# Bilinear field pairs in fp32: each product as three float32r products of split parts, the partial sum scaled in PSUM, engine order written out by hand

## The chip, the cores and the metric

The kernel runs on one NeuronCore of a Trainium2 chip. The metric is the time of one execution on the device in microseconds (us), the median of several runs; less is better. A profile of one execution by the hardware profiler gives the spans, waits and transfers that are read below.

## What is computed

There are 32 fields of 128 numbers for each of 1024 batch rows, and one 128x128 matrix W for each of the 496 unordered pairs of fields. The reference, cut to what matters:

```python
_pairs = np.array(list(itertools.combinations(range(32), 2)))
v_i = inputs[:, I_IDX, :]                  # inputs: 1024 x 32 x 128, float32
v_j = inputs[:, J_IDX, :]
transformed = jnp.einsum('bpd,ped->bpe', v_i, W)   # W: 496 x 128 x 128
return transformed * v_j                   # 1024 x 496 x 128, float32
```

For each pair (i, j) field i is multiplied by the pair's matrix, and the result is multiplied element by element with field j. The output is 496 x 128 x 1024 float32 numbers, 260 MB, and it is by far the largest array.

## The kernel before, in words

Everything is laid out with the 128 embedding positions on the partitions. A pair is one tile of 128 partitions by 1024 batch columns. The host only transposes and permutes; on the chip the kernel walks the pairs in the order of `_pairs` (L20 to L22): j from 1 up, and for each j all i below it, so that each new j needs one new field.

- **Loads.** `load_x` (L49 to L53) brings one field, 512 KB, into a tile that stays for the whole run. `load_w` (L58 to L61) brings a chunk of eight matrices, 512 KB, into one of four buffers. The first few loads of fields go out on SyncE's (SP's) queue, the matrices and the later fields on ScalarE's (ACT's) queue. In the loop, a chunk is asked for three chunks ahead (L76, L77) and a field three groups ahead (L78, L79).
- **Products.** A pair takes a PSUM tile `po` of 1024 columns, two banks (L80, four such tiles), and two matmuls of 512 columns with fp32 operands (L81 to L88). Each of these appears in the profile as two MATMUL records on the PE.
- **Second factor and output.** VectorE (DVE) multiplies the PSUM tile by field j into half of an output tile `ot` (L93), and for every two pairs SP issues one transfer of 1024 KB to HBM (L95). There are six such output tiles. The last two pairs are done in halves (L97 to L100).
- **Order.** Nothing is written out by hand: the order on each engine is that of the program as the tile framework schedules it. The framework sets semaphores between engines from the tiles that an instruction reads and writes. ScalarE and GpSimd (POOL) compute nothing; ScalarE only issues transfers.

Of the kernel before, what the change touches and what calls it, by code (L numbers as in the profile page):

```python
# [1 line left out]

# [4 lines left out]

F32 = mybir.dt.float32
ALU = mybir.AluOpType

P = 128
NF = 32
NQ = NF * (NF - 1) // 2
BT = 1024
HB = 512
WC = 8
OC = 2


def _pairs():  # L20

    return [(i, j) for j in range(1, NF) for i in range(j)]  # L22


@with_exitstack
def kernel(
    ctx: ExitStack,
    tc: tile.TileContext,
    xt: bass.AP,
    wt: bass.AP,  # L30
    out: bass.AP,
):

    nc = tc.nc
    pairs = _pairs()  # L40

    xpool = ctx.enter_context(tc.tile_pool(name="x", bufs=1))
    wpool = ctx.enter_context(tc.tile_pool(name="w", bufs=4))
    opool = ctx.enter_context(tc.tile_pool(name="o", bufs=6))
    ppool = ctx.enter_context(tc.tile_pool(name="ps", bufs=4, space=bass.MemoryType.PSUM))

    x_sb = {}

    def load_x(f, eng, pieces=1):  # L49
        x_sb[f] = xpool.tile([P, BT], F32, tag=f"x{f}", name=f"x_{f}")  # L50
        s = BT // pieces
        for k in range(pieces):
            eng.dma_start(out=x_sb[f][:, k * s : (k + 1) * s], in_=xt[:, f, k * s : (k + 1) * s])  # L53

    nchunk = NQ // WC
    w_sb = {}

    def load_w(c, splits=(0, WC)):  # L58
        w_sb[c] = wpool.tile([P, WC, P], F32, tag="w", name=f"w_{c}")
        for a, b in zip(splits, splits[1:]):  # L60
            nc.scalar.dma_start(out=w_sb[c][:, a:b, :], in_=wt[:, c * WC + a : c * WC + b, :])  # L61

    load_w(0, (0, 1, 3, WC))
    load_x(0, nc.sync, 2)
    load_x(1, nc.sync, 2)
    load_x(2, nc.sync)
    load_w(1)
    load_x(3, nc.sync)
    load_w(2)
    load_x(4, nc.scalar)  # L70
    load_x(5, nc.scalar)

    out_v = out.rearrange("q e b -> e q b")
    ot = None
    for q, (i, j) in enumerate(pairs):
        if q % WC == 0 and q // WC + 3 < nchunk:  # L76
            load_w(q // WC + 3)  # L77
        if i == 0 and 5 < j + 3 < NF:  # L78
            load_x(j + 3, nc.scalar)  # L79
        po = ppool.tile([P, BT], F32, tag="po", name=f"po_{q}")  # L80
        for h in range(0, BT, HB):  # L81
            nc.tensor.matmul(  # L82
                po[:, h : h + HB],
                w_sb[q // WC][:, q % WC, :],
                x_sb[i][:, h : h + HB],
                start=True,
                stop=True,
            )  # L88
        r = q % OC
        if r == 0:  # L90
            ot = opool.tile([P, OC, BT], F32, tag="ot", name=f"ot_{q}")
        if q < NQ - OC:
            nc.vector.tensor_tensor(ot[:, r, :], po[:, :], x_sb[j][:, :], ALU.mult)  # L93
            if r == OC - 1:
                nc.sync.dma_start(out=out_v[:, q - r : q + 1, :], in_=ot[:, :, :])  # L95
        else:
            for h in range(0, BT, HB):  # L97
                s = slice(h, h + HB)
                nc.vector.tensor_tensor(ot[:, r, s], po[:, s], x_sb[j][:, s], ALU.mult)  # L99
                nc.sync.dma_start(out=out_v[:, q, s], in_=ot[:, r, s])  # L100


# [25 lines left out]
```

## Time and profile before

| what | value |
|---|---|
| median of 10 runs | 878.23 us (877.66 to 878.86) |
| the profiled execution, its own time | 878.86 us |
| its span, first to last instruction | 876.2 us |
| mean granted TensorE clock | 0.998 |
| PE busy | 856.8 us, 98% of the span, 1984 matmul records |
| DVE busy | 605.5 us, 69%, 498 instructions |
| POOL busy | 0.2 us |
| moved by DMA | 309.69 MB, mean 353 GB/s |
| read from HBM, written to it | 49.28 MB, 260.05 MB |

A group's line in the profile gives the source line, the engine, the operation, the tiles it writes and reads, their shapes and the count; then the busy time in us with the mean duration of one in ns; then the idle time of the engine just before these instructions and what ended it. The mean duration of a matmul record reaches past the point at which the next matmul starts, because matmuls are pipelined: the busy time divided by the count is the pace, the mean is the latency. "PEld" is the weight load, which runs beside the matmuls. The chain of work that ended last is followed back from the last instruction; "issue" in it is time in which nothing was waited for that the profile shows.

### The profile page before, as it was taken

To read this page: it belongs to the slowest core of one execution; us is meant where nothing else is said; L and a number is where in the kernel's file an instruction comes from. 1 tells how busy PE (TensorE), PEld (TensorE's weight loads), DVE (VectorE), ACT (ScalarE), POOL (GpSimd) and SP (SyncE) were. 2 spreads that over 40 slices of the span, in tenths; PEclk is the share of its full clock that TensorE was granted. 3 is DMA by queue.
4 is the path that set the end of the run, shared out by engine and by line. 5 is a ranking of instruction groups with operands and counts; after the bars stand their busy time and mean duration, and the time that the engine had idled before them with its cause. 6 is when DMAs were issued, how large, how long until landed. Compare 5 with 4: busy or idle time off the path is not lost.

```text
span 876.2 us, 5490 instructions
## 1 busy us (share of the span) xinstructions
PE 856.8 (98%) x1984; PEld 377.2 (43%) x1984; DVE 605.5 (69%) x498; POOL 0.2 (0%) x4
## 2 busy tenths in 40 slices
PE   8997899999999999999999999999999999999997
PEld 3442344444444444444444444444444444444443
DVE  4754677777777777777777777777777777777775
POOL 0000000000000000000000000000000000000000
PEclk9999999999999999999999999999999999999999
DMA  9999999989889898888988989888898988889877
GB/s 344 420 420 420 421 420 415 360 339 355 333 351 342 339 358 333 349 339 340 355 339 345 342 344 351 338 344 342 350 345 338 347 339 353 342 338 352 329 311 296
DMA packets 81898, 309.69 MB, mean 353 GB/s; under 512 B 5584, under 2 KB 5840, under 8 KB 81872
## 3 DMA queue, kind: packets, MB, share of 16 engines
q1 hardware_dynamic: 68624, 262.16, 75.3%
q10 hardware_dynamic: 13248, 47.19, 15.2%
q8 instruction: 15, 0.25, 0.1%
q14 instruction: 11, 0.09, 0.0%
HBM read 49.28 MB, written 260.05 MB: 353 GB/s over the span
## 4 chain that ended last, share of the span: by engine, by line
PE 93%; DMA 6%; DVE 0%; DVEq 0%; issue 0%; SPq 0%
PE po L82 93%; DMA x<-in_xt_dram 3%; DMA w<-in_wt_dram 2%; DMA out_dram<-ot 1%; DVE ot L93 0%; DVE ot L99 0%; DVEq L121 0%; DVEq L93 0%; SPq L95 0%
## 5 line engine op out<-in xcount | busy, mean ns | idle before, releaser
L82 PE MATMUL po<-x,w 128*128 128x512 f32 x1984 | 856.8, 594 | 13.9 <-DVE ot L93 9.9
L93 DVE TENSOR_TENSOR ot<-po,x 128x1024 f32<-128x1024 f32 x494 | 603.0, 1224 | 265.5 <-PE po L82 227.2
L82 PEld LDWEIGHTS po<-x,w 128*128 128x128 f32 x1984 | 377.2, 191 | 492.6 <-issue 470.1
L99 DVE TENSOR_TENSOR ot<-po,x 128x512 f32<-128x512 f32 x4 | 2.6, 686 | 0.9 <-PE po L82 0.9
L115 POOL MEMSET const-bfloat16-1.0<- 128x1 bf16 x1 | 0.1, 101 | 0.0
L115 POOL MEMSET const-uint8-127<- 128x1 uint8 x1 | 0.1, 101 | 0.0
L115 POOL MEMSET const-float32-0.0<- 128x1 f32 x1 | 0.1, 98 | 0.2 <-issue 0.2
L115 POOL MEMSET const-float32-1.0<- 128x1 f32 x1 | 0.1, 98 | 0.0
## 6 DMA issues: line engine op xcount, KB each, us to landing
out_dram<-ot SPq DMA_DIRECT2D x247, 1024.0 KB, 4.6
w<-in_wt_dram ACTq DMA_DIRECT2D x61, 512.0 KB, 4.2
x<-in_xt_dram ACTq DMA_DIRECT2D x28, 512.0 KB, 12.6
x<-in_xt_dram SPq DMA_DIRECT2D x4, 256.0 KB, 4.9
x<-in_xt_dram SPq DMA_DIRECT2D x2, 512.0 KB, 9.6
out_dram<-ot SPq DMA_DIRECT2D x4, 256.0 KB, 3.3
w<-in_wt_dram ACTq DMA_DIRECT2D x1, 320.0 KB, 6.5
w<-in_wt_dram ACTq DMA_DIRECT2D x1, 128.0 KB, 3.7
```

The source lines that it names most:

```text
L82: nc.tensor.matmul(po[:, h : h + HB], w_sb[q // WC][:, q % WC, :], x_sb[i][:, h : h + HB], start=True, stop=True,)
L93: nc.vector.tensor_tensor(ot[:, r, :], po[:, :], x_sb[j][:, :], ALU.mult)
L99: nc.vector.tensor_tensor(ot[:, r, s], po[:, s], x_sb[j][:, s], ALU.mult)
L115: nc = _bacc.Bacc("TRN2", target_bir_lowering=False, num_devices=1)
```

## The change

The new kernel does each fp32 product of 128x128 by 128x512 as three products in float32r, which the change counts as one pass of TensorE each. Of a number it makes a high part h, a rest l, and the difference d = h - l (for the weights, the scales are arranged so that the three parts fit). With eps = 2^-12, the sum of the first two products is scaled by 1 + eps and the third product of the d parts is added.

- **Splitting.** `split_w` works on a chunk of four matrices (512 columns), `split_x` on half a field (512 columns). Each is one ScalarE multiplication (h) and three GpSimd operations: a subtraction, a multiplication by a constant, a subtraction. A field is split once, when it becomes the left factor; for this the order of the pairs is turned round: i from 30 down, and for each i all j above it.
- **Products.** The unit u is half a pair (512 columns, one bank). `first(u)` issues two float32r matmuls into the bank and a ScalarE multiplication of the bank by 1 + eps, in place, in PSUM. `second(u)` issues the third matmul onto the same bank and, after the second half, the DVE multiplication and the output transfer. `second` runs two units behind `first` (LAG). The tile `po` still spans two banks, and there are still four.
- **Native start.** The first 15 pairs (NATIVE = 5: i from 30 to 26) use plain fp32 matmuls as before.
- **Transfers.** All loads, apart from the first two fields, and all outputs now go out on SP's queue. Chunks of W have four matrices (256 KB) and are asked for four chunks ahead. Outputs are single pairs of 512 KB, with five output tiles.
- **Order.** `manual_schedule` fixes each engine's order as written; the splits are handed out, at most one for each pair, from a list sorted by when they are needed.

The core of the diff:

```diff
-WC = 8
-OC = 2
+WC = 4
+EPS = 2.0**-12
+NATIVE = 5
+LAG = 2
+WLEAD = 4
+XLEAD = 3
...
-    return [(i, j) for j in range(1, NF) for i in range(j)]
+    return [(i, j) for i in range(NF - 2, -1, -1) for j in range(i + 1, NF)]
...
-    wpool = ctx.enter_context(tc.tile_pool(name="w", bufs=4))
-    opool = ctx.enter_context(tc.tile_pool(name="o", bufs=6))
+    spool = ctx.enter_context(tc.tile_pool(name="xs", bufs=2))
+    rpool = ctx.enter_context(tc.tile_pool(name="wr", bufs=5))
+    wpool = ctx.enter_context(tc.tile_pool(name="ws", bufs=3))
+    tpool = ctx.enter_context(tc.tile_pool(name="tmp", bufs=2))
+    opool = ctx.enter_context(tc.tile_pool(name="o", bufs=5))
     ppool = ctx.enter_context(tc.tile_pool(name="ps", bufs=4, space=bass.MemoryType.PSUM))
...
+    def split_w(c):
+        raw = w_raw[c].rearrange("p q e -> p (q e)")
+        h, l, d = [wpool.tile([P, WC * P], F32R, tag=t, name=f"{t}_{c}") for t in ("wh", "wl", "wd")]
+        hs = tpool.tile([P, WC * P], F32, tag="t", name=f"whs_{c}")
+        nc.scalar.mul(h, raw, 1.0 - 2.0**-13)
+        nc.gpsimd.tensor_tensor(l, raw, h.bitcast(F32), ALU.subtract)
+        nc.gpsimd.tensor_scalar(hs, h.bitcast(F32), EPS, 1.0, ALU.mult, ALU.mult)
+        nc.gpsimd.tensor_tensor(d, l.bitcast(F32), hs, ALU.subtract)
+        w_s[c] = (h, l, d)
...
+    def split_x(f, a):
+        if a == 0:
+            x_s[f] = [spool.tile([P, BT], F32R, tag=t, name=f"{t}_{f}") for t in ("xh", "xl", "xd")]
+        s = slice(a, a + HB)
+        h, l, d = [t[:, s] for t in x_s[f]]
+        ls = tpool.tile([P, HB], F32, tag="t", name=f"xls_{f}_{a}")
+        nc.scalar.mul(h, x_sb[f][:, s], 1.0 - 2.0**-13)
+        nc.gpsimd.tensor_tensor(ls, x_sb[f][:, s], h.bitcast(F32), ALU.subtract)
+        nc.gpsimd.tensor_scalar(l, ls, 1.0 / EPS, 1.0, ALU.mult, ALU.mult)
+        nc.gpsimd.tensor_tensor(d, h.bitcast(F32), l.bitcast(F32), ALU.subtract)
...
+    ctx.enter_context(tc.manual_schedule())
...
+    def first(u):
+        q, h = divmod(u, 2)
...
+        if h == 0:
+            po[q] = ppool.tile([P, BT], F32, tag="po", name=f"po_{q}")
+        if q < nq0:
+            nc.tensor.matmul(po[q][:, s], w_raw[c][:, q % WC, :], x_sb[i][:, s], start=True, stop=True)
+        else:
+            for t in (0, 1):
+                nc.tensor.matmul(po[q][:, s], w_s[c][t][:, r], x_s[i][t][:, s], start=t == 0, stop=t == 1)
+            nc.scalar.mul(po[q][:, s], po[q][:, s], 1.0 + EPS)
+
+    def second(u):
+        q, h = divmod(u, 2)
...
+        if q >= nq0:
             nc.tensor.matmul(
+                po[q][:, s], w_s[q // WC][2][:, r], x_s[i][2][:, s], start=False, stop=True, skip_group_check=True
             )
...
+        elif h == 1:
+            nc.vector.tensor_tensor(ots[q], po.pop(q), x_sb[j], ALU.mult)
+            nc.sync.dma_start(out=out[q], in_=ots[q])
+
+    for u in range(2 * NQ + LAG):
+        q = u // 2
+        if u % (2 * WC) == 0 and q // WC + WLEAD < nchunk:
+            load_w(q // WC + WLEAD)
+        if u < 2 * NQ:
...
+            first(u)
+        if u >= LAG:
+            second(u - LAG)
+        if u % 2 == 1:
+            ready = [t for t in todo if t[0] <= q]
+            if ready:
+                ready[0][2]()
+                todo.remove(ready[0])
```

## The prediction

> **What bounds the kernel now.** I read the busy times first, then the chain of work that ended last, then the groups, then a table of windows, and last the timeline around the few stalls.
>
> ```profile
> PE 856.8 (98%) x1984; PEld 377.2 (43%) x1984; DVE 605.5 (69%) x498; POOL 0.2 (0%) x4
> PE 93%; DMA 6%; DVE 0%; DVEq 0%; issue 0%; SPq 0%
> L82 PE MATMUL po<-x,w 128*128 128x512 f32 x1984 | 856.8, 594 | 13.9 <-DVE ot L93 9.9
> L93 DVE TENSOR_TENSOR ot<-po,x 128x1024 f32<-128x1024 f32 x494 | 603.0, 1224 | 265.5 <-PE po L82 227.2
> L82 PEld LDWEIGHTS po<-x,w 128*128 128x128 f32 x1984 | 377.2, 191 | 492.6 <-issue 470.1
> ```
>
> TensorE sets the end: 93% of the chain is L82. A pair is four records, 4 x 0.428 = 1.71 us; DVE needs 1.22 us for it and waits for the PE. The windows (span, busy time and count of PE, PEld, DVE, POOL; clock; DMA share; GB/s) show the second limit:
>
> ```profile
> 20.00:40.00 20.00, 20.00 (x48) 8.80 (x47) 14.09 (x13) 0.00 (x0) 1.00 1.03 421
> 80.00:100.00 20.00, 14.90 (x33) 5.75 (x33) 9.85 (x9) 0.00 (x0) 1.00 1.03 420
> 300.00:500.00 200.00, 200.00 (x467) 88.54 (x466) 142.36 (x118) 0.00 (x0) 1.00 0.89 343
> ```
>
> Early on, fields and outputs together hold the DMA at 420 GB/s, and the PE stalls (14.9 us of 20). Later the PE paces everything, the DMA has room (343 GB/s), and 467 records in 200 us give the pace, 0.428 us. From the chain in order of time and the timeline of a stall I take latencies:
>
> ```profile
> 96.62 1.24 DVE ot L93
> 97.86 0.04 issue
> 97.90 772.78 PE po L82 x1800
> 870.68 0.02 issue
> 870.71 0.69 DVE ot L99
> ```
>
> ```profile
> 82.83 3.70 PE L82 MATMUL po<-x,w 128*128 128x512 f32 x8 [1.14 <-DVE ot L93]
> 87.68 2.84 PE L82 MATMUL po<-x,w 128*128 128x512 f32 x6 [1.15 <-DVE ot L93]
> ```
>
> Three numbers come out. A signal from DVE to PE takes 0.04 us, one from PE to DVE 0.02. The drain of a matmul after its last column is 0.594 - 0.428 = 0.166 us. A matmul that begins after a wait shows its weight load: 8 x 0.428 + 0.166 = 3.59 against 3.70, and 6 x 0.428 + 0.166 = 2.73 against 2.84, so 0.11 us.
>
> **What the Trainium skill says.** "FP8 and Floating Point Precision", TensorE Precision Notes: true fp32 takes four passes, reduced fp32 is truncated on reading. "TensorE: Matmul & The Clock Gate", Wait — 56ns, not 53.3ns?: a warm pass of 512 columns is 215.7 ns. The trace agrees with both: two records of 0.428 us are four passes of 0.214. So I put a float32r matmul at 0.214 us; no run here shows one. "SBUF — State Buffer", Who interferes with whom: a DVE instruction with one SBUF input doesn't contend with GpSimd; L166's other input is PSUM, so I leave DVE at 1.22 us. No GpSimd work stands in this trace to confirm it.
>
> **The change, part by part.**
>
> *The products.* Of 496 pairs, 15 stay native; 481 have six matmuls of 0.214 = 1.28 us in place of 1.71. With nothing else this takes 481 x 0.43 = 207 us off the PE. The DMA would then bind: 309.69 MB at 420 GB/s is 737 us.
>
> *The wait that is added.* This decides. `po` is one tile of two banks. In the built program the waits of PE are these for a pair q (h0, h1 its halves): two matmuls of h0; the third matmul of h0 of pair q-1, which waits for the scaling of h1 of q-1; the first matmul of h1, **which waits for the scaling of h0 of the same tile**, though it writes the other bank; its second; the third matmul of h1 of q-1. This holds in all 481 pairs. So LAG gives no cover: between the scaling of h0 and what waits for it stands one matmul. Behind the waiting matmul on the PE queue stand all later ones; ScalarE waits for them for its next scaling, DVE for the third product, SP for DVE.
>
> The scaling on ScalarE isn't in this trace. The skill's price ("ScalarE: Activation LUTs", What ACT_TABLE_LOAD costs: 186 ns + 0.833 ns per element with immediate operands) gives an estimate of 0.61 us for 512. Bounds: 0.43 us (the elements alone) and 0.69 us (the nearest row: DVE's 512-column instruction, above at 870.71). I take 0.61.
>
> A period, from the end of the stream of h1's second matmul to the same point of the next pair: third matmul and two matmuls of the next h0, 3 x 0.214 = 0.64; drain 0.17 and signal 0.04; scaling 0.61; signal 0.04; exposed weight load 0.11 (bounds 0 and 0.19, the mean load); two matmuls of h1, 0.43. Sum **2.05 us**. The third matmul in the gap waits for the previous scaling, which ends at 0.17 + 0.04 + 0.61 = 0.82 us; with 0.15 for signal and load and 0.21 of stream it is done at 1.18, before 1.50 when the scaling of h0 signals: it costs nothing. 481 x 2.05 = **986 us**.
>
> *The splits on ScalarE.* 124 - 3 = 121 chunks and 52 half fields make 173 more ScalarE instructions of 512 columns, 0.61 us each, put after the scaling of an h1 and ahead of that of the next h0. The scaling of h1 ends at 0.82 in the period; the next h0 could be scaled from 0.85. So the whole split lies on the path: 0.58 us. The skill's page says that back-to-back instructions overlap by 0.093 us; twice that leaves 0.39. I take 0.47. Five splits fall into the native start: 168 x 0.47 = **79 us**.
>
> *The splits on GpSimd.* Three operations each. "GPSIMD Engine Reference", Elementwise — side-by-side cycle accounting: 2.6 cycles an element for two inputs at 1.2 GHz, 1.1 us; for one input I take between 0.43 us and this. As an estimate, 3 us a split, 173 x 3 = 519 us beside 1060 us of PE chain: hidden. In the early groups of 6 to 8 pairs 3.5 to 4 splits come per group, 10 to 12 us against 14 to 18 us: still covered; if GpSimd took over 4 us a split, these groups would wait some us each. I put 0, with 20 us at the top of the range.
>
> *Loads and outputs moved to SP's queue.* Now 649 transfers go out there, behind outputs that wait for DVE. A chunk is asked for 16 pairs ahead, about 33 us, against 4.2 us to landing. Chunks have half the bytes per row; outputs are 512 KB. Demand in the steady part is 590 KB per 2.2 us, 268 GB/s against 420: no cost. Five output tiles give 5 x 2.2 = 11 us for a cycle of 1.2 us DVE and about 4.6 us of transfer: no cost. Were the PE at 1.28 us a pair, this cover would be gone and the DMA would bind at 1.4 us.
>
> *Start and end.* The first matmul at 4 us as now; 15 native pairs 26 us, of which the first 6 us run at half pace in this trace (weight loads 0.85 us apart), 3 us more. Up to pair 15 some 15.7 MB are to be moved, 37 us at 420 GB/s, but four PSUM tiles and five output tiles let the PE be ahead of it. I take 34 us. After the last matmul of the second kind come a scaling, a third matmul, a half DVE step and a transfer: 6 us, as against 5.5 now.
>
> *Sum.* 34 + 986 + 79 + 6 = 1105 us of span. The profiled execution took 878.86 us with a span of 876.2, so 2.7 us lie around it; its time is 0.6 us above the median of the runs. 1105 + 2.7 - 0.6 = **1107 us**.
>
> **Rivals.**
>
> *The DMA becomes the bound, and it is faster.* If the scaling were hidden, the period would be the largest of 1.28 (PE), 1.44 (ScalarE: 2.36 instructions of 0.61 us), 1.22 (DVE) and 590 KB at 420 GB/s, 1.40 us: 1.44 x 481 + 40 = 733 us, and with the DMA's own sum of 737 us and 10 us of start and end about 750 us. For it speaks 420 GB/s held over 100 us in this trace; against it, the wait is in the program for every pair. The point: break-even with 878 needs a period of (876 - 40) / 481 = 1.74 us with splits, 1.58 without, so the scaling would have to take 0.14 us. 512 elements allow that only if ScalarE does far more than one a cycle. 4%.
>
> *TensorE falls to half pace.* It would be busy 1.28 of 2.2 us, 58%. At half pace as in the first 6 us: 3 x 0.428 + 0.21 + 0.61 + 0.15 + 0.86 = 3.11 us, the splits then fit in the gap; 481 x 3.11 + 45 = 1541 us. A float32r matmul that takes two passes' time gives the same. For it: a start in which it happens; against it: between 60 and 100 us the PE is busy some 75% with gaps of over 1 us, and its pace afterwards is 0.428 all the same. 9%.
>
> *GpSimd becomes the bound.* This needs more than 1070 / 173 = 6.2 us a split; at 6.8 us it gives 173 x 6.8 + 40 = 1216 us. Nothing in the trace prices it; the skill's figure speaks against it. 4%.
>
> **How the numbers follow.** The forecast (the scaling round trip paces the PE) has 83%. Its own bounds: scaling 0.54 and 0.69 in place of 0.61 give -34 and +38 us; the split's delay 0.39 and 0.58, -13 and +18; the exposed load 0.05 and 0.19, -29 and +38; GpSimd +20. Not all at one end at once: 1050 to 1190. Outside are the fast case, half pace, GpSimd, and a few per cent of the forecast's own. A difference of 0.2% is about what can be told from no change here. Slower 0.95, faster 0.04, same 0.01.
>
> **What would show it.** The chain must alternate between PE at L148, ScalarE at L149 and some L88 and L103. PE's busy time falls to about 650 us of span 1105, and the first matmuls of L148 wait for ScalarE at L149 481 times, about 0.7 us each. ScalarE's mean for 512 columns should be 0.61 us. DMA stays near 280 GB/s, GpSimd near half busy. Wrong would be: a busy time of PE at L148 and L157 far above 0.214 us x count; waits for POOL at the head of the list; or a DMA at 420 GB/s throughout.

## The result, and the profile after

The changed kernel takes 1117.11 us (median of 8 runs, 1115.58 to 1117.81) against 878.39 us before (29 runs): a ratio of 1.2715, 95% interval 1.2704 to 1.2726. It is slower by 239 us; 1107 us was forecast. The profiled execution took 1115.75 us with a span of 1114.0.

From the page of the changed kernel: busy times, the chain by engine and by line, and the groups of the three products, the scaling and one GpSimd operation.

```profile
PE 953.0 (86%) x2946; PEld 515.1 (46%) x2946; DVE 607.5 (55%) x498; ACT 638.0 (57%) x1136; POOL 548.2 (49%) x523
PE 52%; ACT 34%; issue 10%; DMA 3%; ACTq 0%; DVE 0%; POOL 0%; SPq 0%; DVEq 0%
PE po L148 45%; ACT po L149 25%; PE po L157 7%; ACT wh L88 7%; ACT xh L103 3%; DMA x<-in_xt_dram 1%; DMA out_dram<-ot 1%; DMA w<-in_wt_dram 1%; ACTq L149 0%; DVE ot L163 0%; DVE ot L166 0%; POOL xd L106 0%; POOL wl L89 0%; SPq L79 0%; SPq L167 0%
L149 ACT ACTIVATE po<-po 128x512 f32<-128x512 f32 x962 | 560.9, 583 | 451.2 <-PE po L148 430.9
L148 PE MATMUL po<-xh,wh 128*128 128x512 f32 x962 | 430.7, 448 | 121.5 <-ACT po L149 87.3
L157 PE MATMUL po<-xd,wd 128*128 128x512 f32 x962 | 426.0, 443 | 30.3 <-ACT po L149 1.6
L89 POOL TENSOR_TENSOR wl<-w,wh 128x512 fp32r<-128x512 f32 x121 | 155.1, 1282 | 468.6 <-ACT wh L88 463.1
L148 PE MATMUL po<-xl,wl 128*128 128x512 f32 x962 | 380.1, 395 | 0.4 <-POOL wl L89 0.4
```

The PE still looks busy for 86% of the span, but that is the trap of this page. A record lasts until its matmul has drained, so the 0.17 us drain ahead of each wait counts as busy, and so does the 0.11 us of weight load that shows after a wait. The chain says what happens: it was 93% PE, and is now 52% PE and 34% ScalarE, with 10% of time between them in which the chain shows no work. ScalarE is on the chain with the scaling (L149, 25%) and with the high part of the splits (L88 and L103, 10%). Nobody is full: DVE 55%, ScalarE 57%, GpSimd 49%.

The list of waits names the pair that meets at every step (us in total, times, longest):

```profile
PEld po L148 <- ACT po L149: 272.7, 481, 1.1
PEld po L157 <- ACT po L149: 171.5, 363, 0.8
PE po L148 <- ACT po L149: 87.3, 168, 0.7
```

The first line holds the whole finding: 481 waits, one for each three-pass pair, of a product at L148 for the scaling at L149. The waits are shown on the weight load, because the record of the matmul before still covers part of the gap. The third line counts 168 waits that reach past that record: those that a split makes longer.

The timeline of the changed kernel, PE alone, for one period; the first column is the start, the second the time of one record:

```profile
501.49 0.50 PE L148 MATMUL po<-xh,wh 128*128 128x512 f32 x1 [0.52 <-ACT po L149]
501.83 0.39 PE L148 MATMUL po<-xl,wl 128*128 128x512 f32 x1
502.06 0.40 PE L157 MATMUL po<-xd,wd 128*128 128x512 f32 x1
502.29 0.39 PE L148 MATMUL po<-xh,wh 128*128 128x512 f32 x1
502.52 0.40 PE L148 MATMUL po<-xl,wl 128*128 128x512 f32 x1
502.95 0.50 PE L157 MATMUL po<-xd,wd 128*128 128x512 f32 x1
503.59 0.50 PE L148 MATMUL po<-xh,wh 128*128 128x512 f32 x1
```

And ScalarE in the same stretch:

```profile
499.83 0.58 ACT L149 ACTIVATE po<-po 128x512 f32<-128x512 f32 x1 [0.88 <-PE po L148]
500.32 0.62 ACT L88 ACTIVATE wh<-w 128x512 fp32r<-128x512 f32 x1
500.85 0.59 ACT L149 ACTIVATE po<-po 128x512 f32<-128x512 f32 x1
502.32 1.22 ACT L149 ACTIVATE po<-po 128x512 f32<-128x512 f32 x2 [0.88 <-PE po L148]
```

Read it as a relay. At 502.52 the second product of an h0 starts; it has drained at 502.92. Its scaling is the second of the two at 502.32 and ends at 503.54. At 503.59 the first product of h1 starts, in the other bank of the same tile. From 501.49 to 503.59 is a period without a split: 2.10 us. The one before it has a split (500.32) between two scalings and runs 2.49 us, from 499.00 to 501.49. Of the 480 periods 313 lie near 2.10 us and 167 near 2.49.

### The profile page after: what moved, and what is told of

Its sections match the earlier page's. It is cut to its first block, busy times and chain, and to the rows that moved or that the text cites. A ratio compares the mean times of both kernels' runs of the same rounds, so it can differ in the third digit from the quotient of the medians.

```text
span 1114.0 us, 11346 instructions
## 1 busy us (share of the span) xinstructions
PE 953.0 (86%) x2946; PEld 515.1 (46%) x2946; DVE 607.5 (55%) x498; ACT 638.0 (57%) x1136; POOL 548.2 (49%) x523
## 4 chain that ended last, share of the span: by engine, by line
PE 52%; ACT 34%; issue 10%; DMA 3%; ACTq 0%; DVE 0%; POOL 0%; SPq 0%; DVEq 0%
PE po L148 45%; ACT po L149 25%; PE po L157 7%; ACT wh L88 7%; ACT xh L103 3%; DMA x<-in_xt_dram 1%; DMA out_dram<-ot 1%; DMA w<-in_wt_dram 1%; ACTq L149 0%; DVE ot L163 0%; DVE ot L166 0%; POOL xd L106 0%; POOL wl L89 0%; SPq L79 0%; SPq L167 0%
## 5 line engine op out<-in xcount | busy, mean ns | idle before, releaser
L166 DVE TENSOR_TENSOR ot<-po,x 128x1024 f32<-128x1024 f32 x494 | 604.8, 1225 | 502.3 <-PE po L157 482.1
L149 ACT ACTIVATE po<-po 128x512 f32<-128x512 f32 x962 | 560.9, 583 | 451.2 <-PE po L148 430.9
L148 PE MATMUL po<-xh,wh 128*128 128x512 f32 x962 | 430.7, 448 | 121.5 <-ACT po L149 87.3
L157 PE MATMUL po<-xd,wd 128*128 128x512 f32 x962 | 426.0, 443 | 30.3 <-ACT po L149 1.6
L148 PE MATMUL po<-xl,wl 128*128 128x512 f32 x962 | 380.1, 395 | 0.4 <-POOL wl L89 0.4
L148 PEld LDWEIGHTS po<-xh,wh 128*128 128x128 f32 x962 | 179.8, 187 | 294.7 <-ACT po L149 272.7
L157 PEld LDWEIGHTS po<-xd,wd 128*128 128x128 f32 x962 | 180.0, 187 | 257.8 <-ACT po L149 171.5
L148 PEld LDWEIGHTS po<-xl,wl 128*128 128x128 f32 x962 | 181.1, 188 | 21.7 <-POOL wl L89 0.8
L91 POOL TENSOR_TENSOR wd<-wl,whs 128x512 fp32r<-128x512 f32 x121 | 155.4, 1285 | 10.1
L88 ACT ACTIVATE wh<-w 128x512 fp32r<-128x512 f32 x121 | 75.3, 623 | 3.4 <-DMA w<-in_wt_dram 3.4
L103 ACT ACTIVATE xh<-x 128x512 fp32r<-128x512 f32 x52 | 32.3, 622 | 13.2 <-DMA x<-in_xt_dram 13.2
L145 PE MATMUL po<-x,w 128*128 128x512 f32 x60 | 28.1, 627 | 5.0 <-DMA x<-in_xt_dram 5.0
L145 PEld LDWEIGHTS po<-x,w 128*128 128x128 f32 x60 | 11.7, 198 | 20.5 <-issue 15.8
```

Source lines behind the costliest of these rows:

```text
L88: nc.scalar.mul(h, raw, 1.0 - 2.0**-13)
L91: nc.gpsimd.tensor_tensor(d, l.bitcast(F32), hs, ALU.subtract)
L103: nc.scalar.mul(h, x_sb[f][:, s], 1.0 - 2.0**-13)
L145: nc.tensor.matmul(po[q][:, s], w_raw[c][:, q % WC, :], x_sb[i][:, s], start=True, stop=True)
L148: nc.tensor.matmul(po[q][:, s], w_s[c][t][:, r], x_s[i][t][:, s], start=t == 0, stop=t == 1)
L149: nc.scalar.mul(po[q][:, s], po[q][:, s], 1.0 + EPS)
```

## Experiments

The theory: `po` is one tile of two banks, so the scaling of one half counts as a writer of the tile for the product of the other; that wait, once for each pair, sets the period. The rivals: the lag of the third product is too short; the scaling in PSUM as such, or ScalarE's added work as such, holds up the PE.

### e1: a tile for each half

```diff
-    ppool = ctx.enter_context(tc.tile_pool(name="ps", bufs=4, ...))
+    ppool = ctx.enter_context(tc.tile_pool(name="ps", bufs=8, ...))
...
-        if h == 0:
-            po[q] = ppool.tile([P, BT], F32, tag="po", name=f"po_{q}")
+        po[u] = ppool.tile([P, HB], F32, tag="po", name=f"po_{u}")
...
+        nc.vector.tensor_tensor(ots[q][:, s], po.pop(u), x_sb[j][:, s], ALU.mult)
```

> Each half pair gets a PSUM tile of its own (eight tiles of one bank), so the first product of the second half no longer shares a tile with the scaling of the first half; DVE multiplies in halves. Whole-tile wait theory: the waits of L148 for ScalarE go, the period falls from 2.10 us to the largest of PE 6 x 0.23 = 1.38, DVE 2 x 0.69 = 1.38 and DMA 1.40 us, so 750 to 800 us. Rival, the third product follows too soon on the scaling (a lag of two units is too short): over 1050 us, since the lag is unchanged. Rival, the scaling in PSUM as such holds up the PE: over 1050 us.

778.86 us, ratio to before 0.8868 (0.8853 to 0.8882). The same matmuls, scalings, splits and lag take 338 us less. The eight banks of PSUM are the same. From e1's groups, the first product and the scaling:

```profile
L147 PE MATMUL po<-xh,wh 128*128 128x512 f32 x962 | 392.5, 408 | 32.9 <-DVE ot L161 28.1
L148 ACT ACTIVATE po<-po 128x512 f32<-128x512 f32 x962 | 542.4, 580 | 128.6 <-PE po L147 80.7
```

The waits of L147 (L148 before) for ScalarE are gone; what it still waits for is mostly DVE. The rivals fall here: lag, scalings and ScalarE's work are as before. One thing else has changed with the tiles, DVE works in halves; e4 below keeps it whole.

### e2: a longer lag

```diff
-LAG = 2
+LAG = 4
```

> Only LAG goes from 2 to 4. Whole-tile wait theory: no cover is gained, since the first product of a second half still waits for the scaling of its first half issued just before: 1105 to 1125 us. Rival, the lag is too short for the third product: 0.3 to 0.7 us a pair come back, 780 to 970 us.

1118.14 us, one run. Twice the lag gives nothing. Only the third product could use it, and its wait stood in a gap that was there anyway. From e2's waits:

```profile
PEld po L148 <- ACT po L149: 484.9, 481, 1.6
PE po L148 <- ACT po L149: 277.8, 481, 1.1
```

The line of L157 waiting for L149 is gone, and the 481 waits of L148 have grown from 273 to 485 us: the wait has moved, the time has not.

### e3: the high parts made on GpSimd

```diff
-        nc.scalar.mul(h, raw, 1.0 - 2.0**-13)
+        nc.gpsimd.tensor_scalar(h, raw, 1.0 - 2.0**-13, 1.0, ALU.mult, ALU.mult)
```

(and the same in `split_x`)

> The multiplication that makes h is moved from ScalarE to GpSimd in both splits (173 instructions), nothing else. Theory that a split stands ahead of the next scaling on the chain: 168 times 0.39 us go, about 1052 us, and all periods become 2.10 us. Rival, the splits lie beside the chain: 1110 to 1120 us. GpSimd goes from 3.2 to 3.8 us a split, about 660 us in all, and should stay hidden apart from the early short groups (up to 20 us).

1057.42 us, one run: 60 us less. The periods lie at 2.10 us; a few, the longest of 7.36 us at 34 us, are longer, and the PE waits once, 3.8 us, for one of GpSimd's high parts.

### e4: one scaling for a pair, after both halves

```diff
-            nc.scalar.mul(po[q][:, s], po[q][:, s], 1.0 + EPS)
+            if h == 1:
+                nc.scalar.mul(po[q][:, :], po[q][:, :], 1.0 + EPS)
...
-        if u >= LAG:
-            second(u - LAG)
+        if u % 2 == 1 and u >= 3:
+            second(u - 3)
+            second(u - 2)
```

> The tile of two banks stays; the scaling is done once for the pair, over 1024 columns, after the products of both halves, and the two third products follow one pair later. Whole-tile wait theory: no product waits for a scaling issued just before it; M2 to third product is 0.17 + 0.04 + 1.01 + 0.14 = 1.36 us, covered by six matmuls of 0.23; 740 to 800 us. Rival, the scaling in PSUM as such holds up the PE: over 1000 us.

774.89 us, ratio to before 0.882 (0.8805 to 0.8835): the fastest of all by its median, and it keeps the tile of two banks. So the tile's size does no harm in itself; the harm comes of scaling one half between the products of the two. The edit also puts the third products later, but e2 shows that this alone gives nothing; and DVE still multiplies whole pairs here, so its halves in e1 were not needed. From the page of e4, the GB/s of the 40 slices, the chain and the scaling's group, then a window (span; busy time and count of PE, PEld, DVE, ACT, POOL; clock; DMA share; GB/s):

```profile
GB/s 339 377 400 399 400 403 413 414 395 406 396 414 402 413 398 411 402 396 412 402 413 403 406 395 408 408 406 411 400 400 405 403 402 407 407 396 407 403 412 339
PE 42%; DMA 24%; POOL 14%; DVE 8%; issue 7%; SPq 3%; ACT 0%; DVEq 0%; POOLq 0%
L150 ACT ACTIVATE po<-po 128x1024 f32<-128x1024 f32 x481 | 485.8, 1010 | 180.6 <-PE po L148 145.4
40.00:750.00 710.00, 681.49 (x2798) 495.68 (x2796) 570.15 (x466) 544.90 (x631) 527.25 (x496) 1.00 1.02 404
```

ScalarE has left the chain, and the DMA runs at 395 to 414 GB/s from the third slice to the last but one, 404 in the mean of 40 to 750 us, with its engines busy all the time (share 1.02): the transfers are the bound, as in the fast rival of the prediction. The chain is no longer clear about it, with 42% PE and 24% DMA, because the PE is close behind: its six products take 6 x 0.23 = 1.38 us of a mean period of 1.52 (480 periods in 731 us).

### e5: the split at another place on ScalarE

```diff
-        if u % 2 == 1:
+        if u % 2 == 0:
             ready = [t for t in todo if t[0] <= q]
```

> The changed kernel with one edit: a split is handed out after the first half of a pair, so on ScalarE it stands between the scalings of h0 and h1 and no longer between h1 and the next h0. Theory that only its place costs: after the scaling of h0 ScalarE is free for some 0.8 us, the split of 0.6 fits, all periods become 2.10 us, about 1052 us as without splits on ScalarE. Rival, ScalarE's added work as such slows the chain: 1110 to 1120 us.

1052.35 us, one run; the period is 2.10 us also where a split stands in it (only a single one exceeds 2.3 us). The timeline of e5, ScalarE alone:

```profile
499.96 1.22 ACT L149 ACTIVATE po<-po 128x512 f32<-128x512 f32 x2 [0.88 <-PE po L148]
501.09 0.62 ACT L88 ACTIVATE wh<-w 128x512 fp32r<-128x512 f32 x1
502.06 1.22 ACT L149 ACTIVATE po<-po 128x512 f32<-128x512 f32 x2 [0.35 <-PE po L148]
```

The split now fills part of the 0.88 us that ScalarE waits for h1's products. The same work, one position later in the order, costs nothing where it had cost 0.39 us.

### e6 and e9: a third product of 256 columns

```diff
+            s2 = slice(h * HB, h * HB + HB // 2)
             nc.tensor.matmul(
-                po[q][:, s], w_s[q // WC][2][:, r], x_s[i][2][:, s], start=False, ...
+                po[q][:, s2], w_s[q // WC][2][:, r], x_s[i][2][:, s2], start=False, ...
```

e6 is the changed kernel with this edit, e9 is e5 with it.

> The changed kernel with the third product done over 256 of the 512 columns (half of each third product is left out of the result). It asks why a float32r matmul starts 0.23 us after the one before and not 0.214. If the stream of columns sets the pace, the next matmul follows a third product after 0.11 to 0.12 us, the period falls by 0.11 and the time by about 53 us, to 1065. If the weight load (0.19 us each) sets it, the next still follows after 0.2 us or more and the time stays over 1100 us.

1128.45 us, one run, and neither answer fits as it stands. The mean clock is 0.924, and in stretches the PE runs at half pace. At full pace the next matmul does follow a short one after 0.12 us and the period is 1.98 us, so the columns set the pace and not the weight load. The timeline of e6, first in a stretch at full pace and then in one at half pace, and the window of the latter (columns as in e4):

```profile
109.64 0.28 PE L158 MATMUL po<-xd,wd 128*128 128x256 f32 x1
109.75 0.39 PE L148 MATMUL po<-xh,wh 128*128 128x512 f32 x1
109.98 0.40 PE L148 MATMUL po<-xl,wl 128*128 128x512 f32 x1
...
112.57 0.41 PE L158 MATMUL po<-xd,wd 128*128 128x256 f32 x1
112.78 0.63 PE L148 MATMUL po<-xh,wh 128*128 128x512 f32 x1
113.21 0.63 PE L148 MATMUL po<-xl,wl 128*128 128x512 f32 x1
```

```profile
112.00:118.00 6.00, 5.19 (x13) 3.37 (x13) 2.45 (x2) 2.77 (x5) 4.88 (x5) 0.50 0.65 232
```

0.23 us from L148 to L148 in the first part, 0.43 us in the second, where the clock is 0.50. From 36 us on there are 28 such stretches of 3 to 10 us. Every one begins at the end of a gap of 0.57 to 0.64 us between two records, or one period later, and gaps of this length stand only in periods with a split; most of the some 150 such gaps are followed by no loss of pace.

> e5 (splits between the two scalings of a pair) with the third product over 256 columns as in e6, so that no period of 2.49 us is left; half of each third product is left out of the result. e6 showed half the TensorE pace in stretches, its period elsewhere 1.98 us. If the pace falls because the periods with a split are too empty: all periods 1.98 us, a clock of 0.99 or more, about 997 us. If an idle share just above that of the changed kernel is enough: stretches of half pace again, a clock below 0.97 and over 1015 us.

1001.35 us, one run, clock 0.998, periods of 1.97 to 2.00 us but for a few. So the shorter product gives back 51 us against e5's 1052.35, near the 481 x 0.11 = 53 that the period of 1.99 promises. The half pace is gone with the emptier periods that held a split. This fits the first answer, but it rests on one run each of e6 and e9, made on different chips. The length of the gap alone is not the reason: in e2 the PE stands still between records for over 0.8 us 166 times, for 1.1 us at the longest, with 1.38 us of matmuls in a period, and its clock is 0.998.

### e7 and e8: what holds the DMA at 404 GB/s

e7 is e4 with chunks of eight matrices for the loads (the splits still take four), e8 is e4 with the loads on ScalarE's queue.

```diff
-        w_raw[c] = rpool.tile([P, WC, P], F32, tag="w", name=f"w_{c}")
+        t = rpool.tile([P, 2 * WC, P], F32, tag="w", name=f"w_{c}")
+        w_raw[2 * c], w_raw[2 * c + 1] = t[:, :WC, :], t[:, WC:, :]
```

```diff
-            nc.sync.dma_start(out=w_raw[c][:, a:b, :], in_=wt[:, c * WC + a : c * WC + b, :])
+            nc.scalar.dma_start(out=w_raw[c][:, a:b, :], in_=wt[:, c * WC + a : c * WC + b, :])
```

> One scaling per pair as in e4, and the matrices loaded eight at a time again (4 KB rows in place of 2 KB, three buffers in place of five). e4 moved 404 GB/s with the DMA at its full share, where the kernel before held 420. If the short rows cost the difference: 410 to 420 GB/s and 748 to 765 us. If it is the single queue or the mix of reads and writes: within 4 us of e4, 771 to 779 us.

777.10 us, ratio to before 0.8848 (0.8835 to 0.8861); 400 GB/s between 200 and 600 us. The wider rows bring nothing over the whole.

> One scaling per pair as in e4, and all loads issued from ScalarE's queue, so that loads and outputs use two queues as in the kernel before. If one queue holds the DMA at 404 GB/s: up to 420 GB/s and 748 to 765 us. If not: 770 to 785 us, or a little more, since ScalarE waits for the buffers of its loads.

777.41 us, ratio to before 0.8842 (0.8819 to 0.8865), the runs between 774.94 and 782.28; 401 GB/s between 200 and 600 us. Nor does a second queue. What separates 404 from the 420 GB/s of before is left open. One difference stands in the windows: between 20 and 140 us before, 64 pairs of 0.524 MB are 67% of what was moved; between 40 and 750 us in e4, 466 pairs are 85%. So the faster stretch reads more and writes less. Two windows of e7 point the same way (columns as in e4):

```profile
20.00:80.00 60.00, 57.64 (x209) 37.22 (x207) 43.91 (x36) 36.18 (x45) 54.93 (x53) 1.00 1.03 419
80.00:140.00 60.00, 55.99 (x230) 40.60 (x231) 47.22 (x40) 46.00 (x56) 55.43 (x54) 1.00 1.02 402
```

With pairs at 75% of the bytes it is 419 GB/s, with 87% it is 402. The rows may count as well: e4 has 398 GB/s between 40 and 80 us, with 24 pairs, 79%, and e7 has 418 there, with 25, 78%. No run changes the mix alone.

### e10: a scaling of half the columns

```diff
-            nc.scalar.mul(po[q][:, s], po[q][:, s], 1.0 + EPS)
+            s2 = slice(h * HB, h * HB + HB // 2)
+            nc.scalar.mul(po[q][:, s2], po[q][:, s2], 1.0 + EPS)
```

(on top of e5)

> e5 with each scaling over 256 of its 512 columns (the other half is left unscaled in the result): the scaling should take 0.58 - 0.21 = 0.37 us. Theory that the scaling of h0 lies on the chain in full, once for each pair: the period falls from 2.10 to 1.89 us, 481 x 0.21 = 102 us less than e5, about 950 us. Rival, part of the wait is something else that the scaling merely covers (the third product's wait, DVE): less than 60 us come back, over 990 us.

951.87 us, one run: 100.5 us less than e5. From e10's groups, the scaling:

```profile
L150 ACT ACTIVATE po<-po 128x256 f32<-128x256 f32 x962 | 354.0, 368 | 476.5 <-PE po L148 469.9
```

It went from 0.582 to 0.368 us, and 481 x 0.214 = 103 us should go. There are two scalings in a pair, but only one of them is on the chain: with both, twice as much would have come back.

## Why the prediction was right

**The bound and the sign.** The wait that the prediction put at the centre is there 481 times, at the line it named. That it is this wait and no other is shown from several sides: take the shared tile away (e1), or the scaling between the two halves (e4), and 338 to 342 us go; lengthen the lag (e2), and nothing goes; shorten the scaling (e10), and the time follows it nearly one to one.

**The period, 2.05 forecast, 2.10 measured.** By its terms: five matmuls 1.07 us forecast, 5 x 0.23 = 1.15 measured; drain 0.17 and 0.17; scaling 0.61 and 0.58; signals 0.08 and 0.09 (from 502.92 to 503.54 less the scaling of 0.58, and from 503.54 to 503.59); exposed weight load 0.11 and 0.11 (501.49 to 501.83 less 0.23). The measured terms sum to 2.10. Those forecast sum to 2.04; the prediction wrote 2.05, a slip of 5 us in all. The term that was mis-sized is the float32r matmul, taken over from the fp32 pass of 0.214 and 0.08 us too little over five; the scaling gave 0.03 of it back, and the others, measured in the trace of before, held. Over 481 pairs the five hundredths between 2.05 and 2.10 are 24 us too little.

**The splits, 0.47 us each forecast, 2.49 - 2.10 = 0.39 measured.** This is the lower bound of the prediction: the overlap of back-to-back instructions that the Trainium skill ("ScalarE: Activation LUTs", What ACT_TABLE_LOAD costs) gives as 93 ns is in the timeline twice, 499.83 + 0.58 against 500.32, and 500.32 + 0.62 against 500.85. 168 x 0.08 makes 13 us too much. So two errors of opposite sign, +24 and -13 us, leave the forecast closer than its terms were, and that is luck. e3 and e5 confirm the term: 60 and 65 us without it, 168 x 0.39 = 66.

**The signs.** The chain, the 481 waits (272.7 / 481 = 0.57 us each, 0.7 forecast), the DMA and GpSimd came as the prediction said. PE's busy time did not: 953 us, where it had put some 650 and had called a time far above 0.214 us x count a sign of being wrong. Here the sign was badly chosen. The records of a period also hold two drains and two weight loads that no other matmul covers: 6 x 0.23 + 2 x 0.17 + 2 x 0.11 = 1.94 us, times 481 some 930 of the 953 us. The pace itself is 0.23 us, not far above 0.214.

**Start and end.** The first three-pass product starts at 32.5 us, 34 forecast. 2.7 us were put around the span, 1.75 measured.

**What was costed at nothing.** GpSimd takes 1.28 + 0.62 + 1.28 = 3.2 us a split (3 forecast), 548 us in all, and hardly delays anyone: products wait for it 0.4 us at L148. That DVE would not suffer from it (the Trainium skill, "SBUF — State Buffer", Who interferes with whom) holds: 1225 ns beside 548 us of GpSimd work, 1224 without. SP's queue carried 653 transfers (649 by the prediction) at 278 GB/s, and nothing on the chain points to it: DMA has 3% there.

**The rivals.** The fast one was right about what comes next: with the wait gone the DMA binds. It was priced at 750 us with 420 GB/s; e4, with 404, took 775. GpSimd never came near. Half pace did not occur in the changed kernel from 36 us on (clock 0.998), but e6, with less work in the same periods, had it.

## What to carry to other kernels

Where a framework tracks dependencies by tile, an in-place step on one part of a tile is a wait for whatever writes another part next; give each part a tile of its own, or put the in-place step after all its writers. Ahead of any count of saved passes, write down for one period who waits for whom, and look for a round trip between engines that lasts longer than the work left to do meanwhile. On an engine with a fixed order, the place of a side task decides its cost: behind the step that others wait for, a split was free; ahead of that step it cost 0.39 us, 168 times.

## What was not expected of the hardware

- A float32r matmul of 512 columns starts 0.23 us after the one before, not 0.214 as a pass of fp32 does (0.428 for two); with 256 columns it is 0.12 us. It goes with the columns; why it is slower than a pass of fp32 was not found.
- TensorE fell to half pace in e6, though from 36 us to the last pairs the gaps between its records were at most 0.64 us; e2, with gaps of up to 1.1 us, kept the full pace. A period with a split held 4 x 0.23 + 2 x 0.12 = 1.16 us of matmuls in about 2.49 us. The changed kernel and e2, with 1.38 us in 2.49, and e9, with 1.16 us in 1.98, kept the full pace. These shares, 47% against 55% and 59%, fit a limit on the busy share; no run varied it on purpose, and where a limit would lie was not measured.
- The scaling, priced at 612 ns, took 583 from PSUM to PSUM; a high part of a split, from SBUF to SBUF, took 623 for the same 512 columns.
